# A two-layer relational graph network on one core: layer 2's root product in layer 1, twenty tiles of layer 2 on SyncE, the sort's hits in PSUM, and the one-hots of an octet in two instructions

## The chip, the core and the metric

The kernel runs on one core of a Trainium2 chip. The metric is device time in microseconds of one execution, smaller is better. The core has five engines with instruction streams of their own: TensorE (PE in the profile, with its weight loads as PEld), VectorE (DVE), ScalarE (ACT), GpSimd (POOL) and SyncE (SP). [...] DMAs are issued by GpSimd, SyncE and ScalarE; an instruction that waits holds up everything behind it in its engine's stream.

## The reference

12,500 nodes with 128 features, 200,000 edges sorted by their target, 8 relations, two layers. Cut to what matters:

```python
def _rgcn_conv(x, src, dst, et, basis, comp, root, bias):
    W = jnp.einsum('rb,bio->rio', comp, basis)
    xw = jnp.einsum('ni,rio->nro', x, W)
    msgs = xw[src, et]
    seg = dst * N_REL + et
    summed = jax.ops.segment_sum(msgs, seg, num_segments=N_NODES * N_REL)
    cnt = jax.ops.segment_sum(jnp.ones((msgs.shape[0],), x.dtype), seg, ...)
    mean = summed / jnp.maximum(cnt, 1.0)[:, None]
    agg = mean.reshape(N_NODES, N_REL, HIDDEN).sum(axis=1)
    return agg + x @ root + bias
h = x
for l in range(N_LAYERS):
    h = jax.nn.relu(_rgcn_conv(h, src, dst, edge_type, basis[l], comp[l], root[l], bias[l])) + h
x = _layernorm(x + h, axis=-1)
```

The kernel has to bring one row of 128 numbers for each edge and layer, weigh it by one over its segment's count, and add it to its target node; to that come the root product of every node, the bias, the residual and, at the end, the layer norm.

## The kernel before

**Tiles, octets, blocks.** The edges lie in 1563 *tiles* of 128. Eight tiles are an *octet* (`Q = 8`, 196 octets); a *block* is 128 nodes (`NT = 98`), and on average two octets hold a block's edges. All the work is handed to a planner (`Plan`): code calls `pe`, `vec`, `act`, `pool` and `load` in program order, the planner works out the semaphore waits from the cells that each operation names as read and written, and each engine runs its own operations in exactly that order. A cell that belongs to a PSUM bank (`ps`, `py`, `po`, `pt`, `ct`) counts as written by whoever reads it. `load` puts a DMA on SyncE's queue, or on ScalarE's with "ACT".

**Layer 1** (loop over `o`, one octet each) gathers rows of `x`: one GpSimd indirect DMA for each tile into a ring of 7 octet buffers, 5 octets ahead (`gather`, L806). TensorE multiplies each tile with a scaled one-hot (`means`, L1364; VectorE makes the one-hots at L1270), multiplies by the eight relation matrices (`product`, L1396, into bank `y_full`), and places the octet's sums in the columns of a block (`place`, L1427). When a block is complete, `finish` adds what the block before carried over (L1448), makes the next carry with the bias (L1452), applies relu and residual (L1472) into `hT`, and `end` stores the block to `h_d`; `table` multiplies it by layer 2's eight matrices and stores that to `y_d`, the table of layer 2.

**SyncE's tiles.** Some tiles are not gathered by GpSimd: `SINGLES` lists them. `single_lists` stores their byte offsets in DRAM, and `single_rows` lets SyncE load 32 offsets into registers (L755) and issue 16 DMAs of one 512-byte row each (L759), so a tile is 8 parts of 16 rows, with a register load before every second one. The parts are spread over the octets before the tile is used, the first `step + 16` tiles and the last some three octets ahead; two buffers (`hw_b`) alternate. Before the change 24 tiles of layer 1 go this way, one in 56, and none of layer 2.

**The sort.** From octet 96 of layer 1 on, VectorE and TensorE also sort the edges of 62 *routed* octets of layer 2 (every third: 7, 10, ... 190). For each of them `groups_of` makes one-hots of the source's group, `earlier_of` counts on TensorE how many edges of the same group come earlier (bank `ct`), `ranks_of` turns the counts into ranks (L1666, L1667), compares the ranks with 32 slots, the *hits* (L1671, `j3`, half precision in SBUF), and multiplies the hits by three values of each edge (L1674, `v4`, 128 x 768); `slots_of` collects these on TensorE.

**Layer 2** (loop over `q`) gathers rows of `y_d` for the other octets (L806 again) and one short left-over list for each routed octet (`gather_left`, L830). For an octet that is not routed, `slot_hots` makes eight scaled one-hots of 32 columns (L1229) and a placement matrix (L1232), `slot_sums` adds the rows into 16 slots a tile on TensorE (L2026), and `place_sums` puts them in the block (L2059), one octet later. Where an octet opens a block, `place_sums` also adds the block's root product (L2063) from the h rows that `open_block` loaded two octets before it (`hb`, SyncE). The routed octets go through `route`: four steps for each, with one-hots on VectorE (L1868, L1885), products on TensorE (`unit_rows` L1896, `pick_rows` L1918, `add_up` L1938, `relate` L1958), and two loads on SyncE, `fetch` (the group's bits, `lo_d`) and `fetch_rows` (`sc_d`), each of which waits until its buffer is free. The last four octets (`add_rows`, L2083) use wide one-hots, and from octet 190 on a gather also waits for "done", the last sums that TensorE has made.

So SyncE's order in layer 2 is: the parts of a single tile (if any), the loads of the route steps, `open_block`'s load, and now and then x or the output.

Of the kernel before, what the change touches and what calls it, by code (L numbers as in the profile page):

```python
# [301 lines left out]
class Plan:  # L302
# [90 lines left out]
    last = None  # L393
# [37 lines left out]
def ordered_path(  # L431
# [80 lines left out]
    RC, RL = 16, 32  # L512
    SINGLES = [("SP", 0, range(191, NQ * Q - 80, 56))]
    SINGLE = {(l, t): (i, k) for i, (_, l, ts) in enumerate(SINGLES) for k, t in enumerate(ts)}
# [16 lines left out]
    w_d = dram.tile([L, R * D, D], F32, name="w_d")  # L531
    h_d = dram.tile([NT, D, P], F32, name="h_d")

    idx = keep([P, B * P], I32, "idx")
# [682 lines left out]
    def in_quad(q):  # L1217
        return min(Q, T - q * Q)
# [3 lines left out]
    acc, carry, vs, xs, xT, wide = {}, {}, {}, {}, {}, {}  # L1222

    def slot_hots(q):

        t, c = dms2[q] = dm2_r.take()
        o, oc = pl[q] = pl2_r.take()
        i0 = q * Q
        vec(in_turn([lambda i=i: nc.vector.tensor_scalar(  # L1229
            t[:, i, :], cols[:, :2 * K], kr[:, i0 + i:i0 + i + 1], w[:, i0 + i:i0 + i + 1], op0=ALU.is_equal,  # L1230
            op1=ALU.mult) for i in range(Q)]
            + [lambda: nc.vector.tensor_scalar(o, cols, pos[:, q // (2 * R), q % (2 * R):q % (2 * R) + 1], None,  # L1232
                                               op0=ALU.is_equal)]),
            ["cols", "rel", ("wt", q * Q // P), "pos"], new(c) + new(oc))
        plan.mark("DVE")

    def onehot(l, q, g=None):
# [22 lines left out]
        if q < NQ:  # L1260
            if l == 0:
                t = dm_t[:, q % 4 // 2, :].rearrange("p (b t c) -> p b t c", b=2, t=Q)[:, q % 2]
                cells += [("dm", q % 4)]
            else:
                t = dm_t[:, q % 2, :].rearrange("p (t c) -> p t c", t=Q)
                cells += [("dm", 2 * (q % 2)), ("dm", 2 * (q % 2) + 1)] + dm_home_c
            dms[l, q] = (t, list(cells))
            wide, ids = (P, kr) if l == 0 else (2 * P, near)
            for i in range(q * Q, q * Q + in_quad(q)):
                emits.append(lambda i=i: nc.vector.tensor_scalar(  # L1270
                    t[:, i - q * Q, :wide], cols[:, :wide], ids[:, i:i + 1], w[:, i:i + 1], op0=ALU.is_equal,
                    op1=ALU.mult))
            b = q * Q // P
            reads += [("kr" if l == 0 else "near", b), ("wt", b)]
        if g is not None and g >= 0:
# [5 lines left out]
            cells.append(c)  # L1281

        for i, (e, r, c) in enumerate(between):
            emits.insert(2 * i + 1, e)
            reads += r
            cells += c
        between.clear()
        vec(in_turn(emits), reads, cells)
        plan.mark("DVE")
# [145 lines left out]
    def finish(l, k, apart=False):  # L1435
# [3 lines left out]
        def first_step():  # L1439
            a, ac = acc[k] if apart and k + 1 < NT else acc.pop(k)  # L1440
            emits, reads, cells = [], [ac, ("bias_t", l)], []
            if k >= 0:
                vs[k] = a, ac
            if (l, k) == (1, NT - 1):
                return
            if k >= 0:
                t, c = carry.pop(k)
                emits.append(lambda: nc.vector.tensor_add(a[:, :n], a[:, :n], t[:, :n]))  # L1448
                reads.append(c)
            if k + 1 < NT and not apart:  # L1450
# [34 lines left out]
    def table(j):  # L1485
# [171 lines left out]
    def ranks_of(x):  # L1657
        (o3, oc), (vv, vc), (jt, jc), (ct, cc) = hots_of(x), v_b[x % 2], j_b, count_b
# [7 lines left out]
        vec(lambda: nc.vector.tensor_tensor(c3, b3, o3[:, 1:], op=ALU.mult), [bc, oc], [cc])  # L1666
# [7 lines left out]
        vec(lambda: nc.vector.tensor_tensor(  # L1674
            v4, j3[:, :, None, :].to_broadcast([P, Q, 3, CAP]),
            val[:, x, :, :3].unsqueeze(3).to_broadcast([P, Q, 3, CAP]), op=ALU.mult), [jc, val_b[1]], [vc])

# [360 lines left out]
    def place_sums(q, k, opens, last):  # L2038
        t, c = pl.pop(q)
        o, oc = ys.pop(q)  # L2040
        a, ac = acc[k]
        root_in = opens and k >= 0
        reads = [c, oc]
        m = NW if q in ROUTED else P
        if root_in:
            ht, hc = hb[k]
            reads += [hc, ("w", 1, R)]
        more = []
# [9 lines left out]
        def emit():  # L2058
            ins = nc.tensor.matmul(a, o[:m], t[:m], start=opens, stop=last and not root_in and not more)  # L2059
            for rows_m, dm_m in more:  # L2060
                ins = nc.tensor.matmul(a, rows_m, dm_m, start=False, stop=last and not root_in)  # L2061
            if root_in:
                ins = nc.tensor.matmul(a[:, :rows_of(k)], w_sb[:, 1, R, :], ht[:, :rows_of(k)], start=False, stop=last)  # L2063
            return ins
# [4 lines left out]
    def add_rows(q, k, opens, last, between_last=None):  # L2069
# [3 lines left out]
        n = in_quad(q)  # L2073
        root_in = opens and k >= 0
        more = []
        if root_in:
            ht, hc = hb[k][0][:, :rows_of(k)], hb[k][1]
            more += [hc, ("w", 1, R)]

        def some(i0, i1):  # L2080
            def emit():
                for i in range(i0, i1):
                    ins = nc.tensor.matmul(a, t[:, i, :], d[:, i, :],  # L2083
                                           start=(opens and i == 0), stop=(last and i == n - 1))
                    if i == 0 and root_in:
                        nc.tensor.matmul(a[:, :rows_of(k)], w_sb[:, 1, R, :], ht, start=False, stop=False)
                return ins
# [3 lines left out]
        if q == NQ - 2:  # L2091
            for h in range(2):
                pe(some(4 * h, 4 * h + 4), [c + (h,)] + dc + more, [ac, ("done", 1)])
        elif q == NQ - 1:
# [10 lines left out]
        else:  # L2105
            pe(some(0, n), [c + (0,), c + (1,)] + dc + more, [ac, ("done", 1)])
        plan.mark("PE")
# [207 lines left out]
    for o in range(NG - 3):  # L2315
# [95 lines left out]
    batch(None)  # L2411
    end()
    placed(g - 4)
    product(g - 3)
# [35 lines left out]
    for _, b in halves:  # L2450
        b()

    for q in range(AHEAD):
# [152 lines left out]
```

## Time and profile before

| what | value |
|---|---|
| time, median of 3 runs | 3381.97 us (3380.82 to 3383.55) |
| the profiled execution: its own time | 3385.05 us |
| its span, first to last instruction | 3383.1 us |
| PE busy | 2766.1 us, 82% |
| DVE busy | 2270.8 us, 67% |
| ACT busy | 644.9 us, 19% |
| POOL busy | 2547.9 us, 75% |
| mean granted TensorE clock | 0.911 |
| DMA traffic | 289.03 MB, mean 85 GB/s |

How to read it: a group's line gives the source line, engine and operation, output and inputs by name, the count, then busy time and the mean of one in ns, then the idle time of the engine just before these instructions and what ended it. "Issue" is idle time in which the engine waited for nothing that the profile shows. A timeline's line gives start and duration in us, and in brackets the idle time before the instruction with its releaser. Layer 1 lasts until about 1965 us, layer 2 from there to the end. Busy shares are means over both, and the engines' limits differ between them.

### The profile page before, as it was taken

How to read it: one execution, taken by the hardware profiler on the slowest of the kernel's cores; microseconds unless marked ns; L12 is line 12 of the kernel's file. 1: busy time of each engine (PE TensorE's matmuls, PEld its weight loads, DVE VectorE, ACT ScalarE, POOL GpSimd, SP SyncE). 2: the span in 40 equal slices, each digit the busy share in tenths (PEclk: the TensorE clock that was granted, in tenths of full speed). 3: DMA queues.
4: the chain of work that ended last, by engine and by line, in shares of the span. 5: the costliest groups of instructions: out<-in, count | busy, mean ns of one | idle time of the engine just before them, and what ended most of it. 6: DMA issues, size and time to landing. Idle time of an engine off the chain costs nothing.

```text
span 3383.1 us, 73915 instructions
## 1 busy us (share of the span) xinstructions
PE 2766.1 (82%) x27537; PEld 2228.2 (66%) x27537; DVE 2270.8 (67%) x6302; ACT 644.9 (19%) x1627; POOL 2547.9 (75%) x2677
## 2 busy tenths in 40 slices
PE   6777667877667777777776739999999999999995
PEld 4565565656566666766565627777777777777774
DVE  6665454463367888888333238888888888888884
ACT  1211112222122222222222211111111111111110
POOL 7777777777777777777777777777777777777775
PEclk8999879888888888888988879999999999999997
DMA  4242223443322232222333232233223322333222
GB/s 138 56 59 64 57 77 113 132 130 95 89 82 81 75 89 76 82 77 82 115 105 89 88 101 73 72 84 85 78 78 84 84 78 78 84 85 82 78 78 61
DMA packets 171649, 289.03 MB, mean 85 GB/s; under 512 B 66163, under 2 KB 102813, under 8 KB 171285
## 3 DMA queue, kind: packets, MB, share of 16 engines
q0 software_dynamic: 85408, 175.09, 20.3%
q1 hardware_dynamic: 47146, 50.19, 5.0%
q10 hardware_dynamic: 38731, 58.99, 4.9%
q8 instruction: 218, 3.57, 0.5%
q14 instruction: 146, 1.20, 0.1%
HBM read 218.35 MB, written 65.70 MB: 84 GB/s over the span
## 4 chain that ended last, share of the span: by engine, by line
PE 43%; POOL 40%; issue 13%; DVE 2%; DMA 2%; ACT 1%; POOLq 0%; ACTq 0%; SPq 0%; DVEq 0%
POOL rows L806 40%; PE pt L1918 11%; PE y L1938 9%; PE po L1938 7%; PE po L1958 3%; PE s L2059 3%; PE ct L2026 2%; PE s L1364 2%; PE y L1396 1%; DMA rows<-in_x_dram,idx 1%; PE s L2061 1%; DVE dm L1270 1%; PE s L2063 1%; DVE arena L999 1%; PE pt L1495 0%
## 5 line engine op out<-in xcount | busy, mean ns | idle before, releaser
L806 POOL DMA_INDIRECT rows<-in_x_dram,idx x1539 | 1476.8, 960 | 471.3 <-issue 463.5
L806 POOL DMA_INDIRECT rows<-y_d,idy x1067 | 1010.4, 947 | 325.1 <-issue 316.6
L1364 PE MATMUL s<-dm,rows 128*128 128x128 f32 x3078 | 531.6, 344 | 379.6 <-DMA rows<-in_x_dram,idx 351.8
L1364 PEld LDWEIGHTS s<-dm,rows 128*128 128x128 f32 x3078 | 495.2, 252 | 441.1 <-issue 228.1
L1270 DVE TENSOR_SCALAR dm<-cols,kr,w 128x128 f32<-128x128 f16 x1563 | 525.1, 400 | 194.7 <-PE pt L1495 54.8
L1396 PE MATMUL y<-w_sb,sT 128*128 128x128 f32 x3136 | 438.6, 299 | 46.4 <-ACT sT L704 46.4
L1396 PEld LDWEIGHTS y<-w_sb,sT 128*128 128x128 f32 x3136 | 424.6, 217 | 56.4 <-ACT sT L704 55.2
L1918 PE MATMUL pt<-arena,dm 128*32 128x128 f32 x12152 | 391.3, 275 | 2.8 <-DVE dm L1868 2.1
L704 ACT ACTIVATE sT<-s 128x512 f32<-128x512 f32 x391 | 212.3, 594 | 824.8 <-PE s L1364 824.8
L1918 PEld LDWEIGHTS pt<-arena,dm 128*32 128x32 f32 x12152 | 324.6, 110 | 55.2 <-issue 43.0
L1938 PE MATMUL y<-arena,dm 128*128 128x304 f32 x620 | 229.6, 452 | 35.1 <-DVE arena L1885 35.1
L1229 DVE TENSOR_SCALAR sT<-cols,kr,w 128x32 f32<-128x32 f16 x1040 | 238.1, 300 | 7.4 <-PE s L2063 7.3
L1868 DVE TENSOR_TENSOR dm<-arena,cols 128x768 f32<-128x768 f16 x248 | 231.3, 933 | 4.1 <-DMA dm<-sc_d 3.7
L1448 DVE TENSOR_TENSOR po<-po,carry 128x128 f32<-128x128 f32 x98 | 28.8, 294 | 296.9 <-PE pt L1495 104.2
L1938 PE MATMUL po<-arena,dm 128*128 128x304 f32 x620 | 210.3, 421 | 0.0
L704 ACT ACTIVATE dm<-pt 128x256 f32<-128x256 f32 x248 | 95.4, 385 | 578.2 <-PE pt L1918 533.6
L1495 PE MATMUL pt<-w_sb,arena 128*128 128x512 f32 (+1 forms) x326 | 174.5, 618 | 26.3 <-ACT y_row L704 14.9
L704 ACT ACTIVATE y_row<-pt 128x512 f32<-128x512 f32 x165 | 98.5, 597 | 417.8 <-PE pt L1495 153.3
L1938 PEld LDWEIGHTS y<-arena,dm 128*128 128x128 f32 x620 | 102.9, 189 | 88.4 <-DVE arena L1885 35.3
L1885 DVE TENSOR_SCALAR arena<-cols,comp_sb 128x608 f32<-128x608 f16 x155 | 134.9, 902 | 36.1 <-DMA arena<-y_d,arena 36.0
L1938 PEld LDWEIGHTS po<-arena,dm 128*128 128x128 f32 x620 | 118.4, 191 | 41.3 <-issue 0.7
L1885 DVE TENSOR_SCALAR arena<-cols,sel 128x608 f32<-128x608 f16 x155 | 134.8, 902 | 0.0
(327 smaller groups left out, 3583.5 us busy)
## 6 DMA issues: line engine op xcount, KB each, us to landing
hw_SP<-in_x_dram SPq DMA_DIRECT2D x3072, 0.5 KB
y_d<-y_row ACTq DMA_DIRECT2D x96, 512.0 KB
rows<-in_x_dram,idx POOLq DMA_INDIRECT x1539
rows<-y_d,idy POOLq DMA_INDIRECT x1067
arena<-lo_d SPq DMA_DIRECT2D x62, 256.0 KB
x_g<-in_x_dram SPq DMA_DIRECT2D x24, 512.0 KB
h_d<-arena ACTq DMA_DIRECT2D x96, 64.0 KB
out_dram<-x_g SPq DMA_DIRECT2D x12, 512.0 KB
```

The costliest lines, as they stand in the source:

```text
L704: act(lambda: nc.scalar.activation(out_t, in_t, AF.Copy), reads, writes)
L806: ins.append(nc.gpsimd.indirect_dma_start(out=t[:, i - q * Q, :], out_offset=None, in_=table_t, in_offset=bass.IndirectOffsetOnAxis(ap=ids ...
L1229: vec(in_turn([lambda i=i: nc.vector.tensor_scalar(t[:, i, :], cols[:, :2 * K], kr[:, i0 + i:i0 + i + 1], w[:, i0 + i:i0 + i + 1], op0=ALU ...
L1270: emits.append(lambda i=i: nc.vector.tensor_scalar(t[:, i - q * Q, :wide], cols[:, :wide], ids[:, i:i + 1], w[:, i:i + 1], op0=ALU.is_equa ...
L1364: last = nc.tensor.matmul(s_b[i // 4][0][:, i % 4, :], t[:, i, :] if one is None else one[0], d[:, i, :], start=True, stop=True)
L1396: last = nc.tensor.matmul(y[:m], t[:, r, :nt, :].rearrange("p t k -> p (t k)"), w_sb[:, 0, r, :], start=(r == 0), stop=(r == R - 1))
L1495: pe(lambda: nc.tensor.matmul(hb[:n].rearrange("p r d -> p (r d)"), hT[:, j * P:j * P + n], w_sb[:, 1, k * H:(k + 1) * H, :].rearrange("p ...
L1868: emits = [lambda: nc.vector.tensor_tensor(o[:, :3 * n].rearrange("p (j c) -> p j c", j=3), bits[:, None, u * n:(u + 1) * n].to_broadcast( ...
L1885: vec(lambda v=v, o=o: nc.vector.tensor_scalar(o, segs_p, sg[:, v:v + 1], sg[:, NTL + v:NTL + v + 1], op0=ALU.is_equal, op1=ALU.mult), ["n ...
L1918: last = nc.tensor.matmul(b[k * CAP:(k + 1) * CAP, x, :], o[:n, c:c + CAP], hT[:n, j * P:(j + 1) * P], start=jj == 0, stop=jj == SIZE[g] - 1)
L1938: last = nc.tensor.matmul(b.rearrange("p t d -> p (t d)")[:, :SEG], g[:, x * P:(x + 1) * P], o[:, k * SEG:(k + 1) * SEG], start=v == 0, st ...
L1958: pe(in_turn([lambda r=r: nc.tensor.matmul(b[:NW, 0, :], t_s[:, r * NW:(r + 1) * NW], w_sb[:, 1, r, :], start=r == 0, stop=r == R - 1) for ...
```

## The change

Four edits.

1. **Root product of layer 2.** A new `rooting(k)` runs in layer 1, one block for each octet iteration after `product`: one matmul of the block's `hT` with layer 2's root matrix into a second column group of `y_full`, an ACT step that adds the bias, and a store to a new DRAM tile `hr_d` from ScalarE's queue. In layer 2 `open_block(k)` loads `hr_d[k + 1]` (for block 0 also `hr_d[0]`) on SyncE, into a ring of three, and `finish` makes the next carry as a `tensor_add` of that tile instead of adding the bias. `place_sums` and `add_rows` lose the root matmul and their read of `hb`. The last block keeps its own.
2. **SyncE's tiles.** `SINGLES` gets 20 tiles of layer 2: 95, 167, ... 1463, one in 72 tiles, none in a routed octet. GpSimd gathers 20 tiles fewer.
3. **The sort's hits** are written to PSUM (the counts' place in bank `ct`, single precision), and the product with the three values becomes three `tensor_tensor` of 128 x 256.
4. **The one-hots of an octet in layer 2** become two `tensor_tensor` over 128 x 256: a comparison of `cols` with `kr`, and a product with the weights, of which a copy for four octets lies in PSUM (`w_p`). The same form for layer 1 is in the code but switched off.

```diff
-    SINGLES = [("SP", 0, range(191, NQ * Q - 80, 56))]
+    SINGLES = [("SP", 0, range(191, NQ * Q - 80, 56)), ("SP", 1, range(95, (NQ - 12) * Q, 72))]
...
+    hr_d = dram.tile([NT, D, P], F32, name="hr_d")
...
-    j_b = part_of(Q * CAP // 2, "j")
...
+    hr_r = Ring(const, 3, [P, P], F32, "hr")
+    hr, rooted = {}, []
...
+    w_p = bank[:, P + 2 * W:P + 2 * W + 4 * Q].bitcast(F32)
+    in_bank = [None]
+
+    def in_psum(l, q):
+        b = q // 4
+        n = min(T, 4 * Q * (b + 1)) - 4 * Q * b
+        if in_bank[0] == (l, b):
+            return []
+        in_bank[0] = l, b
+        return [lambda: nc.vector.tensor_copy(w_p[:, :n], w[:, 4 * Q * b:4 * Q * b + n])]
+
+    def hots(t, ids, q, n, m):
+        i0, j0 = q * Q, q % 4 * Q
+        return (lambda: nc.vector.tensor_tensor(t, cols[:, None, :m].to_broadcast([P, n, m]),
+                                                ids[:, i0:i0 + n].unsqueeze(2).to_broadcast([P, n, m]),
+                                                op=ALU.is_equal),
+                lambda: nc.vector.tensor_tensor(t, t, w_p[:, j0:j0 + n].unsqueeze(2).to_broadcast([P, n, m]),
+                                                op=ALU.mult))
...
-        vec(in_turn([lambda i=i: nc.vector.tensor_scalar(
-            t[:, i, :], cols[:, :2 * K], kr[:, i0 + i:i0 + i + 1], w[:, i0 + i:i0 + i + 1], op0=ALU.is_equal,
-            op1=ALU.mult) for i in range(Q)]
-            + [lambda: nc.vector.tensor_scalar(o, cols, pos[:, q // (2 * R), q % (2 * R):q % (2 * R) + 1], None,
+        same, scaled = hots(t, kr, q, Q, 2 * K)
+        vec(in_turn([same] + in_psum(1, q) + [lambda: nc.vector.tensor_scalar(o, cols, pos[:, q // (2 * R), q % (2 * R):q % (2 * R) + 1], None,
                                                op0=ALU.is_equal)]),
-            ["cols", "rel", ("wt", q * Q // P), "pos"], new(c) + new(oc))
+            ["cols", "rel", ("wt", q * Q // P), "pos"], new(c) + new(oc) + ["w_p"])
+        vec(scaled, ["w_p"], c if isinstance(c, list) else [c])
...
-                emits.append(lambda: nc.vector.tensor_scalar(nt, a[:, P:], bias_t[:, l:l + 1], None, op0=ALU.add))
+                if l == 1 and k + 1 < NT - 1:
+                    rt, rc = hr.pop(k + 1)
+                    emits.append(lambda: nc.vector.tensor_add(nt, a[:, P:], rt))
+                    reads.append(rc)
+                else:
+                    emits.append(lambda: nc.vector.tensor_scalar(nt, a[:, P:], bias_t[:, l:l + 1], None, op0=ALU.add))
...
+    def rooting(k):
+        n = rows_of(k)
+        b, bc = y_full[0][:, 1, :n], y_full[1]
+        t, c = hr_r.take()
+        pe(lambda: nc.tensor.matmul(b, w_sb[:, 1, R, :], hT[:, k * P:k * P + n], start=True, stop=True),
+           [("h", k), ("w", 1, R)], [bc])
+        plan.mark("PE")
+        act(lambda: nc.scalar.activation(t[:, :n], b, AF.Identity, bias=bias_t[:, 1:2]), [bc, ("bias_t", 1)], [c])
+        plan.mark("ACT")
+        stores.append(lambda: load(hr_d[k][:, :n], t[:, :n], [c], [("hr_d", k)], "ACT"))
...
+    def hits_in(b):
+        return b.rearrange("p t d -> p (t d)")[:, :Q * CAP].rearrange("p (t c) -> p t c", t=Q)
...
-        j3 = jt.bitcast(F16).rearrange("p (t c) -> p t c", t=Q)
+        j3 = hits_in(b)
...
-            op=ALU.is_equal), ["cols", rc], [jc])
-        vec(lambda: nc.vector.tensor_tensor(
-            v4, j3[:, :, None, :].to_broadcast([P, Q, 3, CAP]),
-            val[:, x, :, :3].unsqueeze(3).to_broadcast([P, Q, 3, CAP]), op=ALU.mult), [jc, val_b[1]], [vc])
+            op=ALU.is_equal), ["cols", rc], [bc])
+        vec(in_turn([lambda i=i: nc.vector.tensor_tensor(
+            v4[:, :, i, :], j3, val[:, x, :, i:i + 1].to_broadcast([P, Q, CAP]), op=ALU.mult) for i in range(3)]),
+            [bc, val_b[1]], [vc])
...
+        for j in range(0 if k == 0 else k + 1, min(k + 2, NT - 1)):
+            t, c = hr[j] = hr_r.take()
+            load(t, hr_d[j], [("hr_d", j)], [c])
...
-        root_in = opens and k >= 0
...
-            if root_in:
-                ins = nc.tensor.matmul(a[:, :rows_of(k)], w_sb[:, 1, R, :], ht[:, :rows_of(k)], start=False, stop=last)
...
+                if k < NT - 1:
+                    rooted.append(k)
...
+        if rooted:
+            rooting(rooted.pop(0))
...
+    while rooted:
+        rooting(rooted.pop(0))
+    rooting(NT - 2)
+    for step in stores:
+        step()
+    stores.clear()
```

More of the change, by code (lines that the diff above doesn't have):

```diff
@@ L1268, in onehot @@
             wide, ids = (P, kr) if l == 0 else (2 * P, near)
[L1269 to L1272, printed above, removed]
+            if l == 0 and False:
+                n = in_quad(q)
+                same, scaled = hots(t[:, :n, :wide], ids, q, n, wide)
+                emits += [same] + in_psum(l, q)
+            else:
+                for i in range(q * Q, q * Q + in_quad(q)):
+                    emits.append(lambda i=i: nc.vector.tensor_scalar(
+                        t[:, i - q * Q, :wide], cols[:, :wide], ids[:, i:i + 1], w[:, i:i + 1], op0=ALU.is_equal,
+                        op1=ALU.mult))
             b = q * Q // P
@@ L1281, in onehot @@
             cells.append(c)
+        then = [] if q >= NQ or l or not False else [(scaled, dms[l, q][1])]
         for i, (e, r, c) in enumerate(between):
@@ L1287, in onehot @@
         between.clear()
-        vec(in_turn(emits), reads, cells)
+        vec(in_turn(emits), reads, cells + (["w_p"] if then else []))
+        for e, c in then:
+            vec(e, ["w_p"] + c, c)
         plan.mark("DVE")
@@ L1451, in first_step @@
                 nt, ncell = carry[k + 1] = carry_r.take()
-                emits.append(lambda: nc.vector.tensor_scalar(nt, a[:, P:], bias_t[:, l:l + 1], None, op0=ALU.add))
+                if l == 1 and k + 1 < NT - 1:
+                    rt, rc = hr.pop(k + 1)
+                    emits.append(lambda: nc.vector.tensor_add(nt, a[:, P:], rt))
+                    reads.append(rc)
+                else:
+                    emits.append(lambda: nc.vector.tensor_scalar(nt, a[:, P:], bias_t[:, l:l + 1], None, op0=ALU.add))
                 cells.append(ncell)
@@ L1657, in ranks_of @@
     def ranks_of(x):
-        (o3, oc), (vv, vc), (jt, jc), (ct, cc) = hots_of(x), v_b[x % 2], j_b, count_b
+        (o3, oc), (vv, vc), (ct, cc) = hots_of(x), v_b[x % 2], count_b
         f0, f1, f2, fw, fc = flags(x)
@@ L2041, in place_sums @@
         a, ac = acc[k]
-        root_in = opens and k >= 0
         reads = [c, oc]
         m = NW if q in ROUTED else P
-        if root_in:
-            ht, hc = hb[k]
-            reads += [hc, ("w", 1, R)]
         more = []
@@ L2058, in emit @@
         def emit():
-            ins = nc.tensor.matmul(a, o[:m], t[:m], start=opens, stop=last and not root_in and not more)
+            ins = nc.tensor.matmul(a, o[:m], t[:m], start=opens, stop=last and not more)
             for rows_m, dm_m in more:
-                ins = nc.tensor.matmul(a, rows_m, dm_m, start=False, stop=last and not root_in)
-            if root_in:
-                ins = nc.tensor.matmul(a[:, :rows_of(k)], w_sb[:, 1, R, :], ht[:, :rows_of(k)], start=False, stop=last)
+                ins = nc.tensor.matmul(a, rows_m, dm_m, start=False, stop=last)
             return ins
@@ L2073, in add_rows @@
         n = in_quad(q)
[L2074 to L2078, printed above, removed]
         def some(i0, i1):
@@ L2084, in emit @@
                                            start=(opens and i == 0), stop=(last and i == n - 1))
-                    if i == 0 and root_in:
-                        nc.tensor.matmul(a[:, :rows_of(k)], w_sb[:, 1, R, :], ht, start=False, stop=False)
                 return ins
@@ L2092, in add_rows @@
             for h in range(2):
-                pe(some(4 * h, 4 * h + 4), [c + (h,)] + dc + more, [ac, ("done", 1)])
+                pe(some(4 * h, 4 * h + 4), [c + (h,)] + dc, [ac, ("done", 1)])
         elif q == NQ - 1:
@@ L2105, in add_rows @@
         else:
-            pe(some(0, n), [c + (0,), c + (1,)] + dc + more, [ac, ("done", 1)])
+            pe(some(0, n), [c + (0,), c + (1,)] + dc, [ac, ("done", 1)])
         plan.mark("PE")
@@ L2451, in ordered_path @@
         b()
+    while rooted:
+        rooting(rooted.pop(0))
+    rooting(NT - 2)
+    for step in stores:
+        step()
+    stores.clear()
     for q in range(AHEAD):
```

1 line of the change is left out of this document (removed).

## The prediction

> **What bounds the kernel now.** I read the groups by line first, then GpSimd's timeline, then TensorE's waits at the end, then SyncE's. A gather is one GpSimd DMA of 128 rows, 128 edges.
>
> ```profile
> L806 POOL DMA_INDIRECT rows<-in_x_dram,idx x1539 | 1476.8, 960 | 471.3 <-issue 463.5
> L806 POOL DMA_INDIRECT rows<-y_d,idy x1067 | 1010.4, 947 | 325.1 <-issue 316.6
> 4.58 1.10 POOL L806 DMA_INDIRECT rows<-in_x_dram,idx  x1 [2.33 <-DMA arena<-in_dst_dram]
> ...
> 3363.68 0.94 POOL L806 DMA_INDIRECT rows<-y_d,idy  x1 [0.31 <-issue]
> 985.00:1625.00 640.00, 477.23 (x3718) 433.55 (x3719) 514.29 (x1468) 151.62 (x432) 488.15 (x499) 0.84 0.29 80
> 1640.00:1900.00 260.00, 188.26 (x1032) 154.38 (x1031) 90.56 (x280) 61.62 (x128) 196.58 (x209) 0.86 0.34 102
> 2100.00:3300.00 1200.00, 1194.51 (x16702) 913.32 (x16701) 1026.53 (x2626) 182.85 (x531) 907.46 (x961) 1.00 0.30 81
> ```
>
> The last three rows are stretches of the span: busy time of PE, PEld, DVE, ACT and POOL, then clock, DMA share and GB/s. GpSimd gathers from 4.58 to 3364.6 us, and its idle time between is almost all "issue", about 0.30 us a gather: nothing it waits for. In 2100:3300 one gather costs 1200/961 = 1.249 us. TensorE is busy for 1194.51 of those 1200 us at clock 1.00, so the chain of waits runs through it, but what ends its waits afterwards shows who is later:
>
> ```profile
> 3274.61 0.67 PE L2026 MATMUL ct<-rows,sT 128*32 128x128 f32 x16
> ...
> 3311.17 1.10 PE L2026 MATMUL ct<-rows,sT 128*32 128x128 f32 x16 [2.56 <-DMA rows<-y_d,idy]
> 3321.16 1.07 PE L2026 MATMUL ct<-rows,sT 128*32 128x128 f32 x16 [4.76 <-DMA rows<-y_d,idy]
> 3333.56 1.10 PE L2026 MATMUL ct<-rows,sT 128*32 128x128 f32 x16 [8.90 <-DMA rows<-y_d,idy]
> 3342.45 6.72 PE L2083 MATMUL s<-dm,rows 128*128 128x256 f32 x16 [4.50 <-DMA rows<-y_d,idy]
> 3321.03 0.94 POOL L806 DMA_INDIRECT rows<-y_d,idy  x1 [0.30 <-issue]
> ```
>
> L2026 is `slot_sums`; these are octets 182, 188, 189 and 191. TensorE carries a backlog through layer 2, loses it at octet 188, and then waits for rows: 2.56 + 4.76 + 8.90 + 4.50 = 20.7 us of slack. So **GpSimd bounds both layers**, and TensorE is 20 us from being the bound.
>
> **The sort's hits.** In 985:1625 a gather takes 488.15/499 = 0.978 us, in 2100:3300 907.46/961 = 0.944: 499 x 0.034 = 17 us lost.
>
> ```profile
> 1310.57 0.96 DVE L1674 TENSOR_TENSOR arena<-arena 128x768 f16<-128x768 f16 x1
> 1310.69 1.65 POOL L806 DMA_INDIRECT rows<-in_x_dram,idx  x1 [0.31 <-issue]
> 1308.70 0.42 DVE L1666 TENSOR_TENSOR arena<-ct,arena 128x256 f32<-128x256 f32 x1 [2.09 <-PE y L1706]
> 1309.44 0.95 POOL L806 DMA_INDIRECT rows<-in_x_dram,idx  x1 [0.30 <-issue]
> ```
>
> L1674, both inputs in SBUF, overlaps a gather of 1.65 us; L1666, the same operation with one input in PSUM, lies just before one of 0.95. The change turns L1674 into three 128x256 products whose first input is in PSUM, so I take the whole **-17 us**; the bounds are 0 and -17. VectorE pays 3 x 0.42 for 0.96, 0.3 us an octet, inside its wait of 2.09 us for TensorE there; without that cover it would be 62 x 0.3 = 19 us, were VectorE the bound. The hits share the bank of the counts, so the next counts wait for the products; they wait already for `groups_of`, later on VectorE. [...]
>
> **Twenty tiles fewer on GpSimd.** 20 x 1.249 = **-25 us** of gathers, if nothing else becomes late. Alone it would pass TensorE's slack of 20.7 us.
>
> **The root product.** It goes from `place_sums` to `rooting`.
>
> ```profile
> 2055.27 0.70 PE L2059 MATMUL s<-pl,ys 128*128 128x256 f32 x2
> 2055.80 0.38 PE L2063 MATMUL s<-jmp,w_sb 128*128 128x128 f32 x2
> 2056.12 0.23 PE L1896 MATMUL po<-ident,dm 16*128 16x16 f32 x1
> 1979.79 1.84 DVE L1229 TENSOR_SCALAR sT<-cols,kr,w 128x32 f32<-128x32 f16 x8
> ```
>
> From L2063's start to the next start are 0.32 us: 96 blocks x 0.3 = 29 us off TensorE in layer 2, about what GpSimd gains, so TensorE stays as far behind GpSimd as now. The carry's `tensor_add` replaces a `tensor_scalar` of the same tile: nothing.
>
> ```profile
> PE s L1364 <- DMA rows<-in_x_dram,idx: 351.8, 137, 5.2
> 1973.80 0.22 PE L1206 MATMUL pt<-fails,ones 128*1 128x19 f32 x2 [9.47 <-DVE y_row L2005]
> 2028.31 1.38 PE L1938 MATMUL y<-arena,dm 128*128 128x304 f32 x2 [35.08 <-DVE arena L1885]
> ```
>
> In layer 1, 97 x (0.3 us of PE, one 128x128 step and one DMA issue of ACT) lie in TensorE's 351.8 us of waits for rows and beside a ScalarE that is busy for 151.62 of 640 us: nothing; without that cover they would cost 97 x 0.3 = 29 us. Their 64 KB stores add traffic, but a gather takes 196.58/209 = 0.941 us at 102 GB/s and no more at 81. The last products, at the turn of the layers, fall into TensorE's wait of 9.47 us, and the first carry, which now waits for a load, into that of 35.08. New on SyncE: 97 loads, priced below.
>
> **The one-hots.** Eight L1229 take 1.84 us an octet; two 128x256 operations with a PSUM input are bounded by L1666's 0.42 and, were they as dear as L1674 per column, 0.32: some 0.84 us, plus a 32-column copy every fourth octet. VectorE gains 1 us x 130 octets, but TensorE, busy for 1194.51 of 1200 us, hardly waits for it: at most 5 us, and I take nothing.
>
> **What the 20 tiles cost SyncE.** This decides. One tile is 128 DMAs of one row and four register loads (each serves two parts of 16 rows):
>
> ```profile
> L755 SPq TENSOR_LOAD <-off_d x96: 3512/3756/4675, 190.3 to 1758.5; - x96
> 1084.74 54.08 SPq L759 DMA_DIRECT2D hw_SP<-in_x_dram  x128
> 1226.69 53.48 SPq L759 DMA_DIRECT2D hw_SP<-in_x_dram  x128
> 2035.21 0.32 SPq L701 DMA_DIRECT2D jmp<-h_d  x1
> ...
> 2086.03 0.32 SPq L701 DMA_DIRECT2D arena<-lo_d  x1
> 2086.39 0.43 SPq L701 DMA_DIRECT2D id_k<-h_d  x1
> ...
> 2221.92 0.42 SPq L701 DMA_DIRECT2D id_r<-h_d  x1
> 2222.38 0.44 SPq L701 DMA_DIRECT2D out_dram<-x_g  x1
> SPq L701 <- DVE dm L1874: 481.9, 54, 11.0
> SPq L701 <- PE po L1896: 480.2, 55, 12.3
> SPq L701 <- DVE wide L1472: 110.4, 30, 14.4
> SPq L701 <- DVE comp_sb L1898: 12.5, 1, 12.5
> SPq L701 <- DVE comp_sb L1900: 7.0, 22, 0.4
> ```
>
> (The waits are those of 2100:3300.) The rows of 54.08 and 53.48 us hold three of the four register loads; with the first, 3.76, a tile takes 57.5 us. In layer 1 it has 7 octets, 55 gathers = 69 us; in layer 2 it has 9 octets, three of them routed: 50 gathers x 1.249 = **62.4 us**. SyncE also issues, per 9 octets, 3 `fetch`, 3 `fetch_rows`, 4.5 h blocks, 4.5 of the new root blocks and 1 for x and out: 16, each 0.36 to 0.46 from start to start (2086.03 to 2086.39, 2221.92 to 2222.38), I take 0.41: 6.6 us. Together **64.1 us against 62.4**: SyncE, which now waits for 1092 of 1200 us, runs full and short.
>
> So the sum goes along SyncE. A load of h is in its queue behind the first tile's early parts, and cannot go before 2035.21 (it waits for TensorE's use of `jmp`); 2036 is where it begins without a lead. From there to the last part of the last tile (tile 1463, octet 182, issued in octet 179) it has 157 parts = 19.6 tiles x 57.5 = 1127 us and 59 + 59 + 2 x 88 + 22 = 316 loads x 0.41 = 130 us, ending at 2036 + 1257 = 3293, the rows some 2 us later. `slot_sums(182)` waits for all eight parts: 3295 for 3274.61, 20.4 us late. TensorE is in order, so behind that wait stands everything of layer 2; ScalarE and VectorE wait for TensorE, and GpSimd's gathers from octet 191 wait for "done". On the way to octet 188 the 2.56 us wait and 1 us of root products go: 3311.17 + 20.4 - 3.6 = 3328.0. GpSimd's gather for octet 191 follows 0.7 us behind (its wait is on `slot_sums(188)`): 3328.7 for 3321.03. From there the end is GpSimd's, as now. Net +7.7 in layer 2, -17 in layer 1: -9.3 us. The profiled run took 3385.05 us (span 3383.1, 1.95 around it), 0.09% over the median 3381.97: **3375.7, say 3376**.
>
> SyncE's prices bound it. With loads at 0.36 and tiles at 56 it is 45 us earlier, and GpSimd's sum takes over (next part); with loads at 0.54 (the 108 us that SyncE did not wait in 2100:3300, over some 200 loads) it is 316 x 0.13 = 41 later: 3417.
>
> **Rivals.** (1) **GpSimd stays the bound**: SyncE keeps up, 3385.05 - 25 - 17 = **3343**. For it: SyncE's need and room differ by 3%, less than the spread of one register load (3.51 to 4.68). Against: three quarters of SyncE's new time are issues with a fixed pace. It decides at 62.4 us per nine octets. [...] (2) **Slower**: SyncE's loads of layer 2 are dearer between the row DMAs than the back-to-back pairs; its queue is the clock of layer 2, and each 0.03 us on a load is 9.5 us at the end. At 0.44 the gain is gone; at 0.50 the time is 3376 + 28 = **3404**. For it: the 0.54 above; against: part of that is the pause after a wait. [...] The root product and the one-hots alone move nothing in any case.
>
> **How the numbers follow.** The bound of a measurable change is 0.2%, 3375.2 to 3388.7. SyncE as clock near my prices: 0.55 (3360 to 3392; of it 0.20 faster, 0.24 same, 0.11 slower). GpSimd the bound: 0.25, faster. Dearer SyncE: 0.14, slower. Hits free nothing: 0.06, of it 0.02 faster, 0.01 same, 0.03 slower. Faster 0.47, same 0.25, slower 0.28. The range takes in rival 1 and rival 2: 3340 to 3408.
>
> **What would show it.** Gathers of 0.944 us in the sort: hits right. In layer 2: SyncE without waits, TensorE waiting at `slot_sums` of every ninth octet, to 182, for `hw_SP`, GpSimd waiting for TensorE: this forecast. GpSimd without pauses and no `hw_SP` wait: rival 1. VectorE waiting for `lo_d` or `hr` loads: worse than rival 2.

## The result, and the profile after

| | before | after |
|---|---|---|
| time, median of four runs | 3382.76 us (3380.82 to 3385.01) | 3408.89 us (3407.80 to 3409.69) |
| span of the profiled execution | 3383.1 us | 3406.0 us |
| GpSimd's gathers in layer 2 | 1067 | 1047 |

The changed kernel is slower: 1.0077 times the time before, with a 95% interval of 1.0064 to 1.0089. The forecast was 3376, so 33 us are to be found.

First the groups by line of the page after, and two stretches of its span (busy time of PE, PEld, DVE, ACT and POOL, then clock, DMA share and GB/s), to be laid beside those of before. GpSimd's gathers are now at L809.

```profile
L809 POOL DMA_INDIRECT rows<-in_x_dram,idx x1539 | 1458.1, 947 | 471.5 <-issue 463.2
L809 POOL DMA_INDIRECT rows<-y_d,idy x1047 | 991.0, 947 | 389.9 <-issue 304.3
```

```profile
985.00:1625.00 640.00, 491.23 (x3857) 441.46 (x3858) 532.46 (x1607) 167.99 (x476) 483.53 (x514) 0.86 0.31 86
2100.00:3300.00 1200.00, 1144.42 (x15727) 857.17 (x15729) 869.29 (x1878) 173.42 (x505) 887.83 (x942) 0.98 0.31 84
```

In the sort GpSimd fits 514 gathers into the 640 us that held 499, at 483.53/514 = 0.941 us each: layer 1 is faster. In 2100:3300 it makes 942 where it made 961, 19 fewer; these are about the tiles that SyncE brings in that time, so GpSimd got through as many octets as before and gained nothing. Its idle time in layer 2 is no longer all "issue": 389.9 - 304.3 = 86 us are waits. TensorE, busy for 1194.51 us before, is busy for 1144.42. The waits of 2000 to 3406 us name what is late (total, times, longest, in us):

```profile
POOL rows L809 <- PE ct L2076: 76.1, 18, 45.7
DVE dm L1918 <- DMA arena<-lo_d: 66.5, 21, 6.8
PE ct L2076 <- DMA hw_SP<-y_d: 51.5, 17, 6.5
```

TensorE stands in `slot_sums` (L2076) for the rows that SyncE brings, 17 times for 51.5/17 = 3.0 us; VectorE stands for the fetches, which are in the same SyncE queue; GpSimd stands for TensorE. What SyncE itself waits for in 2100:3300, where its waits were 1092 us before, begins with these rows, the longest totals:

```profile
SPq L704 <- DVE arena L1935: 2.0, 5, 0.9
SPq L704 <- DVE sel L1949: 1.6, 2, 1.1
SPq L704 <- PE pt L1968: 1.0, 1, 1.0
```

With the shorter ones these waits come to 12.5 us, each at most 1.1: SyncE issues almost without a pause. And the chain of waits in 2100:3300, by line, first before, then after (the view shows both rows only this far):

```profile
by line: PE pt L1918 28.4%; PE y L1938 23.0%; PE po L1938 19.3%; PE po L1958 8.2%; PE s L2059 8.0%; PE ct L2026 5.6%; PE s L2061 2.1%; PE s L2063 1.6%; POOL rows L806 1.3%; PE po L2166 0.8%; PE po L1896 0.8%; issue 0.5%; DVE x_g L2174 0.4%;
```

```profile
by line: SPq L762 19.6%; PE pt L1968 14.3%; PE y L1988 10.8%; PE po L1988 9.0%; SPq L758 8.6%; issue 6.4%; PE po L2008 5.2%; PE s L2105 5.1%; PE ct L2076 4.0%; SPq L704 3.2%; DVE dm L1918 2.2%; DVE arena L1935 2.0%; DMA hw_SP<-y_d 1.7%; PE 
```

L762 is SyncE's row DMAs, L758 its register loads, L704 its other loads: together 31% of a chain in which SyncE had no place before. Most of the rest of the chain is TensorE work. The last part of the last tile, and what follows it, gives the size:

```profile
2016.75 0.35 SPq L704 DMA_DIRECT2D jmp<-h_d  x1
2017.16 0.43 SPq L704 DMA_DIRECT2D hr<-hr_d  x1
2017.68 5.12 SPq L762 DMA_DIRECT2D hw_SP<-y_d  x16
...
3307.37 5.07 SPq L762 DMA_DIRECT2D hw_SP<-y_d  x16
```

```profile
3313.56 0.54 PE L2076 MATMUL ct<-rows,sT 128*32 128x128 f32 x11 [2.34 <-DMA hw_SP<-y_d]
3313.85 0.27 PE L2076 MATMUL ct<-hw_SP,sT 128*32 128x128 f32 x1
...
3346.84 0.66 PE L2076 MATMUL ct<-rows,sT 128*32 128x128 f32 x16
3347.83 0.94 POOL L809 DMA_INDIRECT rows<-y_d,idy  x1 [45.68 <-PE ct L2076]
```

SyncE's run without longer pauses goes from 2016.75 to 3307.37 + 5.07 = 3312.4, which is 1295.7 us. Octet 182's `slot_sums` can go at 3313.6, octet 188's goes at 3346.84, and GpSimd, which stood for 45.68 us, gathers octet 191 at 3347.83.

### The profile page after: what moved, and what is told of

Read it like the earlier page. It is cut to its first block, busy times and chain, and to the rows that moved or that the text cites. A ratio compares the mean times of both kernels' runs of the same rounds, so it can differ in the third digit from the quotient of the medians.

```text
span 3406.0 us, 79010 instructions
## 1 busy us (share of the span) xinstructions
PE 2774.6 (81%) x27537; PEld 2216.3 (65%) x27537; DVE 2155.8 (63%) x5695; ACT 679.5 (20%) x1724; POOL 2509.7 (74%) x2657
## 4 chain that ended last, share of the span: by engine, by line
POOL 34%; PE 29%; issue 14%; SPq 13%; DVE 6%; DMA 4%; ACT 1%; POOLq 0%; ACTq 0%; DVEq 0%
POOL rows L809 34%; SPq L762 8%; PE pt L1968 6%; PE y L1988 5%; PE po L1988 4%; SPq L758 3%; PE s L1392 2%; PE po L2008 2%; PE s L2105 2%; PE ct L2076 2%; PE y L1424 2%; DMA rows<-in_x_dram,idx 1%; SPq L704 1%; DVE dm L1295 1%; DVE dm L1918 1%
## 5 line engine op out<-in xcount | busy, mean ns | idle before, releaser
L809 POOL DMA_INDIRECT rows<-in_x_dram,idx x1539 | 1458.1, 947 | 471.5 <-issue 463.2
L809 POOL DMA_INDIRECT rows<-y_d,idy x1047 | 991.0, 947 | 389.9 <-issue 304.3
L1392 PE MATMUL s<-dm,rows 128*128 128x128 f32 x3078 | 508.5, 334 | 354.9 <-DMA rows<-in_x_dram,idx 337.4
L1392 PEld LDWEIGHTS s<-dm,rows 128*128 128x128 f32 x3078 | 473.5, 242 | 413.9 <-issue 225.2
L1968 PE MATMUL pt<-arena,dm 128*32 128x128 f32 x12152 | 402.6, 280 | 2.6 <-DVE dm L1918 1.6
L1968 PEld LDWEIGHTS pt<-arena,dm 128*32 128x32 f32 x12152 | 333.5, 112 | 72.1 <-issue 64.5
L1918 DVE TENSOR_TENSOR dm<-arena,cols 128x768 f32<-128x768 f16 x248 | 231.8, 935 | 74.3 <-DMA arena<-lo_d 66.5
L2076 PE MATMUL ct<-rows,sT 128*32 128x128 f32 x2040 | 90.9, 290 | 58.8 <-DMA hw_SP<-y_d 51.5
```

Of the source, the lines that this page charges most:

```text
L809: ins.append(nc.gpsimd.indirect_dma_start(out=t[:, i - q * Q, :], out_offset=None, in_=table_t, in_offset=bass.IndirectOffsetOnAxis(ap=ids ...
L1392: last = nc.tensor.matmul(s_b[i // 4][0][:, i % 4, :], t[:, i, :] if one is None else one[0], d[:, i, :], start=True, stop=True)
L1918: emits = [lambda: nc.vector.tensor_tensor(o[:, :3 * n].rearrange("p (j c) -> p j c", j=3), bits[:, None, u * n:(u + 1) * n].to_broadcast( ...
L1968: last = nc.tensor.matmul(b[k * CAP:(k + 1) * CAP, x, :], o[:n, c:c + CAP], hT[:n, j * P:(j + 1) * P], start=jj == 0, stop=jj == SIZE[g] - 1)
L2076: last = nc.tensor.matmul(m0[i // 2 * 2 * K:(i // 2 + 1) * 2 * K, :], d[:, i, :], t[:, i, :] if one is None else one[0], start=i % 2 == 0, ...
```

## The experiments

Eleven kernels. Theory S says that SyncE's issuing sets the pace of layer 2 (is its "clock") and that the whole loss is there. Theory T says that another part of the change costs by itself: the carry that now waits for a load, the one-hots, or each tile by disturbing what runs beside it. The ratios are to the kernel before, run on the same chip.

| run | time, us | ratio, 95% interval |
|---|---|---|
| e1: all but the 20 tiles | 3366.68 | 0.9941, 0.9925 to 0.9958 |
| e2: 15 tiles | 3350.69 | 0.9897, 0.9880 to 0.9913 |
| e3: root loads on ScalarE | 3363.49 | 0.9932, 0.9916 to 0.9949 |
| e4: hits alone | 3367.96 | 0.9945, 0.9929 to 0.9962 |
| e5: hits, 15 tiles | 3353.07 | 0.9916, 0.9899 to 0.9932 |
| e6: h and root loads on ScalarE | 3334.80 | 0.9863, 0.9846 to 0.9879 |
| e7: the fetches on ScalarE too | 3334.47 | 0.9859, 0.9843 to 0.9876 |
| e8: hits, 20 tiles | 3362.76 | 0.9943, 0.9926 to 0.9959 |
| e9: e8 with h loads on ScalarE | 3348.54 | 0.9903, 0.9886 to 0.9919 |
| e10: e6 with the old one-hots | 3333.60 | 0.9859, 0.9843 to 0.9876 |
| e11: 16 registers a load | 3450.65 | one run |

**The tiles taken out (e1).**

```diff
-    SINGLES = [("SP", 0, range(191, NQ * Q - 80, 56)), ("SP", 1, range(95, (NQ - 12) * Q, 72))]
+    SINGLES = [("SP", 0, range(191, NQ * Q - 80, 56))]
```

> The changed kernel with the 20 tiles of layer 2 given back to GpSimd (SyncE brings single rows in layer 1 only); hits in PSUM, root product ahead and two-instruction one-hots stay. Theory S (SyncE is the clock of layer 2; nothing else in the change costs): SyncE has about 13 us of loads per nine octets and idles, GpSimd is bound again, and only the sort's gain is left: 3385 - 18 = 3366 us (3362 to 3371); GpSimd waits for TensorE's slot_sums less than 5 us in 2000 to 3360 us, against 76 us in the changed kernel. Rival T (the carry that now waits for a load from DRAM, or the new one-hots, hold the chain up by themselves): 3385 us or more, and the waits for lo_d and of GpSimd for TensorE stay.

Measured 3366.7. GpSimd's waits in layer 2 of e1, by the group on the page, are 325.4 - 318.1 = 7 us, and the view of waits puts only 0.3 of them to `slot_sums`, where the changed kernel has 76.1:

```profile
L809 POOL DMA_INDIRECT rows<-y_d,idy x1067 | 1012.2, 949 | 325.4 <-issue 318.1
```

```profile
POOL rows L809 <- PE ct L2076: 0.3, 1, 0.3
```

Theory T falls for the carry and the one-hots: both are in this kernel and it loses nothing to them. The 42 us between e1 and the changed kernel come with the tiles.

**The hits alone (e4).** The edit is the one in `ranks_of`, with `hits_in`, and the removal of `j_b`.

> The kernel before with the sort's hits in PSUM and nothing else of the change. Theory (the product of two SBUF inputs slows the gathers beside it): gathers of 0.94 us in place of 0.98 in the sort, 3383 - 17 = 3366 us (3363 to 3369). Rival (the gather is slow there for another reason, or the gain is lost at the turn of the layers): 3380 to 3384.

Measured 3368.0, and the stretch of the sort in e4 has 484.04/512 = 0.945 us a gather. The timeline of e4 shows the place:

```profile
985.00:1625.00 640.00, 481.83 (x3780) 434.88 (x3781) 530.45 (x1600) 155.14 (x439) 484.04 (x512) 0.85 0.30 83
```

```profile
1310.80 1.09 DVE L1676 TENSOR_TENSOR arena<-ct,arena 128x256 f16<-128x256 f32 x3
1311.16 0.95 POOL L805 DMA_INDIRECT rows<-in_x_dram,idx  x1 [0.30 <-issue]
```

The three products whose first input is in PSUM overlap a gather that takes 0.95 us; the single product of two SBUF inputs overlapped one of 1.65. The other gathers agree. In the trace of before, 43 gathers begin more than 0.05 us after the start of an L1674; each of them ends 1.77 to 1.79 us after that start, however early it began, and together they take 18 us more than 43 gathers of 0.945. In e4, 65 gathers begin under the new products and none takes more than 0.96.

The edit changes the place, the precision and the size of the product at once. Another product of the kernel before separates these: `compare` (L1868) has 128 x 768 elements too, but one of its inputs, `nodes_p`, lies in the PSUM bank `cols`:

```profile
2233.42 0.94 DVE L1868 TENSOR_TENSOR dm<-arena,cols 128x768 f32<-128x768 f16 x1
2233.50 0.94 POOL L806 DMA_INDIRECT rows<-y_d,idy  x1 [0.30 <-issue]
```

Of 168 gathers that begin under it the longest takes 0.957 us, so size alone does not slow a gather. The same holds for L1686, 128 x 1024 with half precision written and one input in `cols` (59 gathers, at most 0.952). Of these three products L1674 alone has two SBUF inputs. The hits are then worth 18 us, and e1 against e4 (0.9941 and 0.9945) says that root product and one-hots add nothing measurable to them where GpSimd is the bound.

**Fifteen tiles (e2).**

```diff
-    SINGLES = [("SP", 0, range(191, NQ * Q - 80, 56)), ("SP", 1, range(95, (NQ - 12) * Q, 72))]
+    SINGLES = [("SP", 0, range(191, NQ * Q - 80, 56)), ("SP", 1, range(95, (NQ - 12) * Q, 96))]
```

> The changed kernel with 15 tiles of layer 2 in place of 20: one every 12 octets instead of 9, same first tile. Theory S: SyncE needs 58.4 us for a tile and 21 loads x 0.48 = 10 us per 12 octets, 68 us of the 84 us that GpSimd needs for them (67 gathers x 1.249); it keeps up, and GpSimd gains 15 gathers: 3385 - 18 - 19 = 3348 us (3344 to 3355), with no hw_SP wait of more than 3 us on TensorE after 2200 us. Rival T (the cost goes with the number of tiles, each tile disturbs gathers or loads by itself, about 43 us for 20): 3366 + 15/20 x 43 = 3398 us.

Measured 3350.7, 58 us less than with 20 tiles. After 2200 us TensorE has no wait for `hw_SP`. A cost that goes with the number of tiles would have left 3398. It is a threshold: at one tile in 12 octets SyncE keeps up, and against e1, on the same chip, the 15 tiles bring 16 of the 18.7 us that their gathers take; at one in 9 it does not keep up, and the five tiles more cost 58 us.

**The price of the loads (e3).**

```diff
-            load(t, hr_d[j], [("hr_d", j)], [c])
+            load(t, hr_d[j], [("hr_d", j)], [c], "ACT")
```

> The changed kernel with 20 tiles, but the 97 loads of the root blocks are issued by ScalarE and no longer by SyncE. Theory S with the prices measured in the changed kernel's trace (a load 0.48 us, a root load 0.51): SyncE has 97 x 0.51 = 49 us less to issue and is still the clock, since 58.4 + 11.5 x 0.47 = 63.8 us per nine octets is over GpSimd's 62.4: 3409 - 49 = 3360 us (3352 to 3370). If the price of my prediction, 0.41, were right and the tiles were the mis-sized term: 3409 - 40 = 3369. Rival T (the wait is that of the carry for data from DRAM, not SyncE's issue time): 3400 to 3415.

Measured 3363.5, 45.4 us less than the changed kernel, or 49 by the two ratios. SyncE's run begins at 2016.7 in both, and its last part ends at 3260.73 + 5.08 = 3265.8 instead of 3312.4. Of the 97 loads 88 lie in that run: 46.6 us for 88 are **0.53 us a root load**, the dearer of the two prices offered (0.41 and 0.51). TensorE still waits for SyncE's rows:

```profile
3260.73 5.08 SPq L762 DMA_DIRECT2D hw_SP<-y_d  x16
```

```profile
PE ct L2076 <- DMA hw_SP<-y_d: 22.6, 10, 4.6
DVE dm L1918 <- DMA arena<-lo_d: 38.6, 14, 5.3
```

The data of the root blocks still come from DRAM and the carry still waits for them, so it was the issuing and not the round trip. VectorE's waits for `lo_d`, 66.5 us before the edit, shrink, and are gone in e6 below, although nothing about the fetches was changed in either: they were late because they stood in SyncE's queue.

**More off SyncE (e6, e7).** The h blocks' load gets the same "ACT" in e6; the two fetches as well in e7.

> The changed kernel with 20 tiles, both the loads of the h blocks and of the root blocks issued by ScalarE. SyncE needs 58.4 + 7 x 0.44 = 61.5 us per nine octets, under the 62.4 of GpSimd: 2017 + 19.6 x 58.4 + 140 x 0.42 = 3221 for its last part, before GpSimd's own octet 182 (3232). Theory S: GpSimd bound, 3385 - 18 - 25 = 3342 us (3338 to 3351). Rival (ScalarE, in order, stands in waits for buffers before the loads and holds up its copies for TensorE): 3360 or more, with TensorE waiting for ScalarE.

> As the run before it, with the fetches for the routed octets (lo_d, sc_d) on ScalarE too, so that SyncE has the 20 tiles and some 22 other loads. Theory S: GpSimd is the bound either way, 3342 us (3338 to 3351), no more than the run before gives. Rival: in the kernel before, SyncE stood 11 us in each of 54 waits for a buffer of these fetches; on ScalarE such waits would stand ahead of the copies that TensorE needs: 3360 to 3400.

Measured 3334.8 and 3334.5. In e6 SyncE's last part starts at 3216.36; at the end TensorE waits for gathered rows again, as in the kernel before, and GpSimd waits for almost nothing. From the timeline and from the waits of e6:

```profile
3216.36 5.09 SPq L762 DMA_DIRECT2D hw_SP<-y_d  x16
3288.59 1.11 PE L2076 MATMUL ct<-rows,sT 128*32 128x128 f32 x16 [9.39 <-DMA rows<-y_d,idy]
```

```profile
POOL rows L809 <- PE ct L2076: 0.9, 3, 0.3
ACT dm L707 <- DMA hr<-hr_d: 36.1, 17, 3.2
```

GpSimd is the bound again and all 20 gathers are gained. The sum of 3342 was 7 us too high; 4 us of that are the chip, whose kernel before took 3381.4, and the other 3 I have not traced. The rival's worry, ScalarE standing in waits ahead of its copies, is there and harmless: ScalarE waits 36.1 us for `hr` loads in 2000:3300 of e6, and TensorE does not wait for it. That e7 gives no more than e6 says that the remaining loads had room on SyncE. (The 11 us in its expectation is the longest of those 54 waits; their mean is 481.9/54 = 8.9.) **e6 beats both kernels.**

**What root product and one-hots are worth (e5, e8, e9, e10).** e5, e8 and e9 are the kernel before with the hits in PSUM and tiles: 15 (the line of e2), 20, and 20 with the h loads on ScalarE. e10 is e6 with the eight `tensor_scalar` of an octet again.

> The kernel before with the hits in PSUM and 15 tiles of layer 2 for SyncE, without the root product ahead and with the old one-hots. My prediction said that the root product and the one-hots move nothing by themselves; TensorE had 20.7 us of slack and the 15 gathers take 18.7. If both are worth nothing: 3349 us (3346 to 3355), as with all parts and 15 tiles (3351). If TensorE or VectorE needs them: 3357 us or more, with TensorE's waits for rows near the end gone.

> The kernel before with the hits in PSUM and 20 tiles of layer 2 for SyncE, without the root product ahead (so without its 97 loads on SyncE) and with the old one-hots. Theory S: SyncE is the clock with 58.4 + 11.5 x 0.47 = 63.8 us per nine octets, as with the root loads on ScalarE (3363): 3363 to 3372, TensorE's extra 29 us lying beside SyncE's time. Then the root product as it was made costs 3409 - 3365 = 44 us here. Rival (TensorE without the relief is so far behind that the two add up): 3375 to 3395.

> Hits in PSUM, 20 tiles for SyncE, the loads of the h blocks on ScalarE; no root product ahead, old one-hots. SyncE has room (61.5 of 62.4 us per nine octets), so this tells what root product and one-hots are worth once SyncE is no longer the clock. Theory: TensorE is then the bound, its slack of 20.7 us being less than the 25 us that GpSimd gains; with 15 tiles and no root product it gave 28.4 us in all, and more tiles can give it nothing: 3381 - 28 = 3353 us (3347 to 3358), against 3335 with both edits, which are then worth 18 us. Rival (they are worth nothing even here): 3335 to 3340.

> All of the change with h and root loads on ScalarE (3335 us), but layer 2's octet one-hots as before, ten instructions' worth in place of two and a copy. VectorE is busy 1 us more per octet, 130 octets. Theory: VectorE does not bound TensorE, so at most 5 us: 3335 to 3340 us. Rival: TensorE waits for the one-hots, and the gain of the run with neither edit missing comes from these: 3345 us or more.

e10 took 3333.6, the same as e6: the one-hots are worth nothing, although they free VectorE of 951.86 - 850.74 = 101 us in 2100:3200 (e10, then e6; the third pair of numbers after the stretch is VectorE's):

```profile
2100.00:3200.00 1100.00, 1095.30 (x15397) 821.96 (x15395) 951.86 (x2449) 171.09 (x494) 831.36 (x881) 1.00 0.32 88
```

```profile
2100.00:3200.00 1100.00, 1095.30 (x15390) 822.37 (x15389) 850.74 (x1843) 170.84 (x494) 831.60 (x881) 1.00 0.33 88
```

e9 took 3348.5, 14 us more than e6 and 15 more than e10, from which it differs only in where the root product is made; so with 20 tiles and SyncE free **the root product is worth 14 us**. The chain of waits in 2800:3300 of e9 is TensorE's:

```profile
by line: PE pt L1920 28.0%; PE y L1940 23.1%; PE po L1940 19.4%; PE po L1960 8.4%; PE s L2061 8.1%; PE ct L2028 5.7%; PE s L2063 2.1%; PE s L2065 1.6%; POOL rows L805 1.3%; PE po L2168 0.8%; PE po L1898 0.8%; issue 0.5%; DVE x_g L2176 0.4%
```

In e5, too, GpSimd waits for `slot_sums` (L2028 there), 9.2 us in all, though with 15 tiles only; but the intervals of e5 and e2 overlap, and the 2 us between their times are not shown to be a difference.

```profile
POOL rows L805 <- PE ct L2028: 9.2, 6, 7.6
```

e8 took 3362.8, at the lower edge of what theory S said, but not by the road it said: its SyncE ends at 3256.80 + 5.07 = 3261.9, and in the waits of TensorE no `hw_SP` appears. There are waits for the h loads instead:

```profile
3256.80 5.07 SPq L758 DMA_DIRECT2D hw_SP<-y_d  x16
```

```profile
PE s L2061 <- DMA id_r<-h_d: 7.0, 4, 3.0
```

With the root product in its old place TensorE needs the h blocks, which queue behind SyncE's parts, and it has no reserve to catch up. On e8's chain in 2100:3300 SyncE has 6.2 + 2.9 + 0.8 = 10% and TensorE most of the rest:

```profile
by line: PE pt L1920 23.9%; PE y L1940 19.7%; PE po L1940 16.5%; PE s L2061 7.1%; PE po L1960 7.0%; SPq L758 6.2%; PE ct L2028 4.8%; SPq L754 2.9%; issue 2.0%; PE s L2063 1.8%; PE s L2065 1.4%; SPq L700 0.8%; PE po L2168 0.7%; PE po L1898 0
```

Moving those loads (e9) brings 14 us. So in the changed kernel the root product brought 97 loads that cost some 45 us (e3), and relieved an engine that was waiting for SyncE anyway: without it and its loads the kernel takes 3363 (e8).

**What a register load costs (e11).**

```diff
-                        a = c * RC % RL
+                        rl = RL if l == 0 else RC
+                        a = c * RC % rl
...
-                                off_d[i][k:k + 1, c * RC:c * RC + RL], engines=[engine_of[e]],
+                                off_d[i][k:k + 1, c * RC:c * RC + rl], engines=[engine_of[e]],
```

> The changed kernel with the row offsets of layer 2 loaded into 16 registers at a time, eight register loads a tile in place of four. If a load has a fixed price (3.93 us whatever its size), SyncE needs 19.6 x 4 x 3.9 = 306 us more and, being the clock, the kernel takes about 3715 us. If the price goes with the registers (0.12 us each), nothing changes: 3405 to 3420.

Measured 3450.7 in one run, 42 us over the changed kernel: neither expectation. The register loads, first those of 32 in the changed kernel's layer 2, then all of e11, 96 of 32 and 160 of 16 (shortest, median and longest in ns):

```profile
L758 SPq TENSOR_LOAD <-off_d x78: 3528/3767/5541, 2023.2 to 3297.5; - x78
```

```profile
L759 SPq TENSOR_LOAD <-off_d x256: 1893/2188/12938, 195.9 to 3341.9; - x128
```

42 us over 19.6 tiles are 2.1 us a tile. A tile's four loads of 32 take 4 x 3.9 = 15.7 us, so eight of 16 take 17.9, or 2.23 each; in the trace the 160 loads of 16 take 2.16 in the mean. That is about 0.5 us fixed and 0.107 us a register. The price goes nearly with the registers; if it goes on so, an estimate from two sizes in one run of e11, larger batches would save little.

## Why the prediction was wrong

**Where it held.** The hits: -17 forecast, 18 measured (e4), with the gathers at 0.941 us. SyncE starts layer 2 at 2016.75, which is 2036 less the 17 us of layer 1 and 2 more. That SyncE becomes the clock, issues almost without waits, makes TensorE wait for `hw_SP` every ninth octet until 182, and GpSimd for TensorE: all of it as the forecast's own test had it. From octet 182 to GpSimd's gather of octet 191 it gave 3328.7 - 3295 = 33.7 us; measured are 3347.83 - 3313.6 = 34.2.

**The step that failed: SyncE's sum of 1127 + 130 = 1257 us.** It took 1295.7, and these 39 us are more than the whole error of 33; an earlier start (2 us) and an end that is shorter after octet 191, 3406.0 - 3347.83 = 58.2 for 3383.1 - 3321.03 = 62.1, take some back. Both terms were low; the figures that follow are counted over the changed kernel's trace, from the start of each instruction to the start of the next:

- The loads, 0.41 forecast: the 313 that lie in the run took 151 us, 0.48 each, 21 us more than the 130. Of these 21, 12.8 us are short waits for buffers, which the sum put at nothing; without them a load is 0.44. I had taken the middle of the spacings 0.36 and 0.46. The rows after show which is which: 2016.75 to 2017.16 is a first load after a part, 0.41; 2017.16 to 2017.68 is a root load ahead of a part, 0.52. The change adds the dear kind.
- The tiles, 57.5 forecast, took 1143.6/19.6 = 58.3: 17 us more than 1127. I priced them by two rows of layer 1, 54.08 and 53.48, and the median register load, 3.76. The row DMAs came out as in those rows; the 78 register loads took 3.93 in the mean, which is 13 of the 17 us. Summed over the trace of before, the 1922 row DMAs and 60 register loads from 500 to 1500 us took 881 us from start to start, 58.7 a tile; that mean was to be had.

Three per cent of a sum (39 of 1257), on a queue that is full, decided the sign. The need was forecast at 64.1 us per nine octets against 62.4 of room; it was 1295.7/19.6 = 66, and the lag that builds up is paid at the end. The working also gave 3417 as the time with dear loads, but the range that I stated stopped at 3408, short of it.

**The rivals.** The second (dearer loads, 3404 at 0.50) is what came; it had the right mechanism, but held the loads alone to be dear, and they came to 0.48 with their waits. I gave it 0.14, although the working had a spread up to 0.54. The first (SyncE keeps up, 3343) would have needed five tiles fewer (e2) or the nine h and root loads per nine octets off its queue (e6). Against the first, 16 one-row DMAs took SyncE 5.12 us to issue, and issuing 97 loads from ScalarE instead saved some 45 us (e3). That the hits free nothing, a chance of 0.06, falls with e4: 0.945 us a gather in the sort, where it was 0.978. The gathers that begin under L1674 took up to 1.72 us; those under L1868, with one input in PSUM, at most 0.957.

**Smaller points.** I wrote that VectorE waiting for `lo_d` would mean worse than rival 2. It did wait, 66.5 us, and the time is 5 us over rival 2; these waits are the same late queue seen from another engine and no second cost: they fall to 38.6 in e3 and are gone in e6. That the root product and the one-hots "alone move nothing in any case" held where GpSimd is the bound (e1 against e4) and, with the root loads off SyncE, beside a full SyncE queue (e3 against e8); the one-hots were worth nothing in e10 either. For the root product it was too strong: once GpSimd gains 25 us, TensorE's slack of 20.7 is gone, and the root product is worth 14 us (e9 against e6). My own sum had both numbers, and I did not put them together for the case in which SyncE keeps up. They give only 25 - 20.7 = 4 of the 14 us; where the rest comes from is not shown.

## What to carry to other kernels

A queue that becomes the clock is to be priced as a queue: count every issue in it, take the mean over all of a kind and not a median or a clean pair of rows, add its short waits, and compare need with room; within a few per cent the sign is open, and one step less of load (15 tiles, or the loads on an idle engine's queue) is safer than the last tile. When an edit that relieves one engine pays with issues on another, look at which of the two is full: here the same loads cost some 45 us on SyncE, and on ScalarE nothing that TensorE waited for. A relief that moves nothing today can be needed by the next edit, as the root product was at 20 tiles once SyncE was free.

## What the hardware showed that was not expected

A register load on SyncE goes nearly with its registers: 3.9 us for 32, 2.2 for 16. A DMA of one row costs SyncE 5.12/16 = 0.32 us in a part and 837.0/2512 = 0.33 over its whole run, and a load that follows another 0.46 to 0.52. A gather of GpSimd that begins under a product of two SBUF inputs (L1674) took up to 1.72 us and ended 1.77 to 1.79 us after the product's start; under two products of similar size with one input in PSUM (L1868, L1686) it took at most 0.957.
